# A third weight tile for the projections, loads one product further ahead, and two moved steps, in an encoder and decoder layer on one core

## The chip, the core and the metric

The kernel runs on 1 core of one Trainium2 chip. It is one program in which five engines work beside each other and wait for each other by semaphores: TensorE (PE, matrix products and transposes), VectorE (DVE), ScalarE (ACT), GpSimd (POOL) and SyncE (SP). SP only issues transfers: every transfer of this kernel is issued on SP, in the order in which the program writes them, and a transfer that waits for something holds back all those behind it. The metric is the device time of one execution in microseconds (us); of several runs the median is given. Everything is float32.

## The reference

The reference is one transformer layer pair with relative position biases, cut here to what is computed:

```python
x = src                                    # ctx_1024, (2, 77, 512)
n = ln(x, n1); x = x + mha(n, n, enc_in, enc_out, enc_bias)       # 16 heads of 32
x = x + relu(ln(x, n2) @ ff1.T + b1) @ ff2.T + b2                 # 512 -> 2048 -> 512
memory = x
y = tgt                                    # x, (2, 2048, 512)
n = ln(y, n1); y = y + mha(n, n, sa_in, sa_out, self_bias + causal)
y = y + mha(ln(y, n2), memory, ca_in, ca_out, cross_bias)
y = y + relu(ln(y, n3) @ ff1.T + b1) @ ff2.T + b2
```

The large part is the causal self-attention over 2048 tokens in two batches. The encoder works on 77 tokens only.

## The kernel before

**Two phases.** The decoder's 2 x 2048 tokens are cut into 8 blocks of 512 tokens (batch b, block m; x = 0 to 7 counts them through). The first phase does the self-attention of all blocks, and beside it the whole encoder, and the cross-attention of the very first block. The second phase does cross-attention and feed-forward of the eight blocks; it is a stream of products whose weights come through a ring of 16 tiles.

**Units and slots.** The first phase is cut into 128 units: a unit is 128 query rows of one group of four heads. A block has 16 units (4 groups by 4 row tiles); block x begins at unit 16x. For each unit, PE makes the scores in pieces of up to 512 keys (L374), DVE brings them from PSUM to SBUF, adds the bias to the last two tiles of keys and takes the maxima (L383, L390, L400), ACT takes the exponentials (L405), PE transposes them (L425), DVE and ACT copy the transposes out (L429, L431), and PE multiplies them with the values (L442). At the end of a unit the main loop calls `slot(n + 1)` (L1179), which runs the extra work hung on that slot, in this order: the entries of `light[n]`, then the jobs of `jobs[n]`, each with `load_next()` in front of it, then the entries of `late[n]`. So the program order of every engine, and of the transfers on SP, is written out by hand through the slot numbers.

**The products of the projections.** Queries, keys and values of a block are made by jobs: `q_job` and `k_job` (L216, L227) take a 512 x 128 piece of the weights; from the second block of a batch on, keys and values are made by seven products of 256 x 256 quarters instead of eight (`part_job`, L990; the table `PARTS` names for each product the weight's quarter, or a sum of quarters S1 to S4 kept in DRAM, and the tokens' quarter, or a sum T1 to T4). Below, k6 of block 6 is the sixth such product for the keys. The order of the products of a block x > 1 that starts at slot u is: q0 at u-5, k1 k6 at u-4, k7 k4 at u-3, k2 k5 at u-2, k3 v1 at u-1, v6 v7 at u, v4 v2 at u+1, then q1, v5 v3, q2 and q3 up to u+5. Block 1 has three in slot 17: v7, v4 and v2. Each of these products has a weight tile `wqk` of 128 x 512 f32 (256 KB), with two buffers in turn. The values of a batch's first block and the output projections use another, single weight tile of 1 MB (`wbig`) and count as jobs without a small tile.

**When a weight is loaded.** All jobs stand in one queue. In front of each job the loop `load_next` (L1127 to L1133) issues loads for the jobs that follow: up to job `ran + 2` (`ran` is the job about to run; a little further at the start), and no further than that two small tiles are in use from `ran` on. With two buffers, the load of a product is therefore written just ahead of the product before it, and has to wait until the product two before it has been read by PE.

**The encoder's steps.** `encoder()` (L489) yields 28 steps, one a slot. Step 15 centers the rows and adds the output bias row `row` on POOL (`add_row`, L632), and then loads the next row, `ca_bv`, into the same tile (`load_row`, L526), which waits for POOL to have read it. It is at the end of slot 16. Step 16, at the end of slot 17, turns the normed rows on PE (L554). The row `ca_bv` is read by step 27 (L748).

**The first cross block.** `first_cross()` (L858) spreads the first block's cross-attention over the slots 65 to 95. Its third layer norm writes each of four row tiles turned into one tile `slab` on ACT (L784, step 20 + 3t), and `store` (L920) sends the slab to `nT3_d` and the rows to `y1` in the same step, so in slots 85, 88, 91 and 94.

**A row tile.** `bv`, a tile of 2 KB per partition, holds the output bias of the cross-attention in the second phase (`early_loads`, L1217, slot 123; used through `norm_stages`, L776). Two `wqk` buffers serve as `o_sums` there, once the projections are done.

Of the kernel before, what the change touches and what calls it, by code (L numbers as in the profile page):

```python
# [17 lines left out]
P = 128  # L18
# [36 lines left out]
def tile_encoder_decoder(ctx: ExitStack, tc: tile.TileContext, ins, out):  # L55
# [103 lines left out]
    with (  # L159
# [12 lines left out]
        wbt = ac.tile([P, NC, D], F32, name="wbig")  # L172
        pts_all = ac.tile([P, 8, HC * P], F32, name="pts")
        oT_all = ac.tile([P, 6, TB * P], F32, name="oT")
        bv = ac.tile([P, D], F32, name="row_sa_bv")
        bo = ac.tile([P, D], F32, name="row_dec_sa_out_b")
        psum = ps.tile([P, 8, 512], F32, name="psum")
        count = {"bank": 0, "banks": 7, "pts": 0, "oT": 0, "mm": 0}
# [17 lines left out]
        wbig, xs, xr = {}, {}, {}  # L196

        def small_w(c0, name="dec_sa_in_wT"):
            w = sb.tile([P, NC, P], F32, name="wqk", tag="wqk", bufs=2)
            nc.sync.dma_start(w, wchunk(name, c0, P))  # L200
            return w

# [286 lines left out]
        def encoder():  # L489
# [218 lines left out]
            def stage():  # L708
                for b in range(B):
                    keep[b] = center(b)  # L710
                add_row()
                load_row("ca_bv")

            yield stage
            yield lambda: [turned(b, keep.pop(b), "n2") for b in range(B)]

            def first(i):
                project(ws["1", i], relu, i * NC)
# [139 lines left out]
        def first_cross():  # L858


            plan = {}

            def at(slot, f):
                plan.setdefault(slot, []).append(f)

            o = 2 * HC * MB
            ys = [pp[:, o + t * D : o + (t + 1) * D] for t in range(TB)]
            qT = pp[:, o + 2048 : o + 4096].rearrange("p (g n) -> p g n", n=MB)
            prs = [pp[:, o + 4096 + i * H * S : o + 4096 + (i + 1) * H * S] for i in range(2)]
            o += 4096 + 2 * H * S  # L870
            kTc = pp[:, o : o + NC * S].rearrange("p (c k) -> p c k", k=S)
            vc = pp[:S, o + NC * S : o + NC * S + D]
            slab = pp[:, o + NC * S + D : o + NC * S + 2 * D].rearrange("p (c n) -> p c n", n=P)
            assert o + NC * S + 2 * D <= 12288
            nT = pp[:, HC * MB : 2 * HC * MB].rearrange("p (c n) -> p c n", n=MB)
            wq, wo = vv[:, 8:12, :], vv[:, 12:16, :]
            rows = {"dec_ca_out_b": kT[:, 0, 3 * MB :], "dec_ff2_b": kT[:, 3, 3 * MB :]}
            oT, xn = kT[:, 1, 3 * MB :], kT[:, 2, 3 * MB :]

            def pts(g):  # L880
                return kT[:S, g, 2 * MB : 3 * MB]

            def loads():
                for t in range(TB):
                    nc.sync.dma_start(ys[t], y1[0][0][:, t, :])
                for n, row in rows.items():
                    i = _ROWS.index(n)
                    nc.sync.dma_start(row, ins["rows"][i : i + 1, :].to_broadcast([P, D]))
                nc.sync.dma_start(wq, wchunk("dec_ca_in_wT", 0))
                nc.sync.dma_start(kTc, ckT_d[:, :, :S])  # L890
                nc.sync.dma_start(vc, cv_d[:, 0, :])

            def more_loads():
                for i in range(2):
                    bias_tile(prs[i].rearrange("p (h k) -> p h k", k=S), 2, P, S, 255 - P * i)
                nc.sync.dma_start(wo, wchunk("dec_ca_out_wT", 0))

            at(0, loads)
            at(5, more_loads)
            for t in range(TB):  # L900
                y = lambda t=t: ys[t]
                fs = norm_stages(
                    y, "n2", rows["dec_ca_out_b"], lambda: xn, lambda t=t: nT[:, :, ts(t, P)]
                )
                for k, f in zip((0, 1, 2, 1), fs):
                    at(1 + t + k, f)
            for g in range(NC):
                at(7 + g, lambda g=g: q_group(g, wq[:, :, ts(g, P)], nT, qT[:, g, :]))
            for t in range(TB):
                y = lambda t=t: ys[t]  # L910
                fs = attend_stages(
                    lambda g, t=t: qT[:, g, ts(t, P)], kTc, vc, y, t < 2, prs[t % 2], pts, lambda: oT, wo
                )[:7]
                for k, f in zip((0, 1, 2, 2, 4, 5, 6), fs):
                    at(11 + 3 * t + k, f)
                fs = norm_stages(y, "n3", rows["dec_ff2_b"], lambda: xn, lambda: slab)
                for k, f in zip((0, 1, 2, 1), fs):
                    at(18 + 3 * t + k, f)

                def store(t=t):  # L920
                    nc.sync.dma_start(nT3_d[:, :, ts(t, P)], slab)
                    nc.sync.dma_start(y1[0][0][:, t, :], ys[t])

                at(20 + 3 * t, store)
            return plan


# [62 lines left out]
        def part_job(kind, b, m, i):  # L990
            name, by = PARTS[i]

            def load():
                w = sb.tile([P, NC, P], F32, name="wqk", tag="wqk", bufs=2).rearrange("p c o -> p (c o)")
                w = w.rearrange("p (c o) -> p c o", c=2)
                if name[0] == "S":
                    src = sa_d[kind][int(name[1]) - 1].rearrange("p (c o) -> p c o", c=2)
                else:
                    src = quarter("dec_sa_in_wT", int(name[1]) - 1, int(name[0]) - 1, sa_from[kind])
                nc.sync.dma_start(w, src)  # L1000
                return w

            def place(to):
                r, c = int(to[0]) - 1, int(to[1]) - 1
                if kind == "k":
                    return kT[:, 2 * r : 2 * r + 2, m * MB + c * TOK : m * MB + (c + 1) * TOK]
                return vv[:, m * TB + 2 * c : m * TB + 2 * c + 2, ts(r, TOK)]

            def run(w):
                n, mm = of_nT(b, m, by), bank()  # L1010
                left, right = (w, n) if kind == "k" else (n, w)
                for f in range(2):
                    for c in range(2):
                        nc.tensor.matmul(
                            mm[:, ts(f, TOK)], left[:, c, ts(f, P)], right[:, c, :], start=c == 0, stop=c == 1,
                        )
                got = mm.rearrange("p (f n) -> p f n", f=2)
                d = {to: place(to) for to in ("11", "12", "21", "22")}
                if i == 1 and kind == "k":
                    for f in range(2):  # L1020
                        nc.scalar.activation(
                            d["11"][:, f, :], got[:, f, :], AF.Identity, bias=vec("dec_sa_in_b", NC + f)
                        )
                elif i == 1:
                    nc.scalar.copy(d["11"], got)
                elif i == 6:
                    ve.tensor_tensor(d["12"], got, d["11"], ALU.add)
                elif i == 7 and kind == "k":
                    for f in range(2):
                        ve.scalar_tensor_tensor(  # L1030
                            d["22"][:, f, :], got[:, f, :], kstep[:, f : f + 1], d["12"][:, f, :], ALU.add, ALU.add
                        )
                elif i == 7:
                    ve.tensor_tensor(d["22"], got, d["12"], ALU.add)
                elif i == 4:
                    ve.tensor_tensor(d["21"], got, d["22"], ALU.add)
                else:
                    for to in ADDS[i]:
                        ve.tensor_tensor(d[to], got, d[to], ALU.add)

            return load, run, True
# [84 lines left out]

        def load_next():  # L1127

            while len(loaded) < min(len(queue), ran[0] + (5 if ran[0] < 4 else 3)):
                ahead = [queue[i][2] for i in range(ran[0], len(loaded) + 1)]  # L1130
                if sum(ahead) > 2:
                    break
                loaded.append(queue[len(loaded)][0]())  # L1133

# [81 lines left out]

        def early_loads():  # L1217
            nc.sync.dma_start(nTt, nT3_d)
            row_into(bv, "dec_ca_out_b")
            for o in range(2):  # L1220
                o_sums.append(sb.tile([P, NC, P], F32, name="wqk", tag="wqk", bufs=2).rearrange("p c o -> p (c o)"))

        def last_loads():
            t = sb.tile([P, MB], F32, name="q", tag="q", bufs=3)
# [10 lines left out]
                t = sb.tile([P, HC, 2 * P], F32, name="bias", tag="bias", bufs=2)  # L1235
                qT.append(t.rearrange("p (g a) k -> p g (a k)", g=2))

        xt_ring = []
        light[len(units) - 5].append(early_loads)
        light[len(units) - 1].append(last_loads)  # L1240

# [333 lines left out]
        def cross(x):  # L1575
# [8 lines left out]

            for t in range(TB):
                fs = norm_stages(
                    lambda t=t: y_of(x, t), "n2", bv, place("xt"), lambda t=t: nT2[:, :, ts(t, P)]
                )
                for k, f in zip((0, 2, 4, 11), fs):
                    plan[t + k].append(f)  # L1590
# [225 lines left out]
```

## Time and profile before

Three runs took 2823.34, 2816.31 and 2821.03 us, the median is 2821.03 us. The profiled execution took 2821.11 us; its span, from the first to the last instruction of the program, is 2819.2 us. So some 1.9 us lie around the span.

| engine | busy, us | share of the span |
|---|---|---|
| PE | 2771.8 | 98% |
| DVE | 1886.7 | 67% |
| ACT | 1440.2 | 51% |
| POOL | 915.1 | 32% |

The mean granted clock of TensorE is 0.992 of full speed, and the transfers move 129 GB/s over the span. A line such as `PE L1014 MATMUL psum<-xr,wqk 128*128 128x256 f32 x8 [1.74 <-DMA wqk<-in_dec_sa_in_wT_dram]` in the list by time reads: eight matmuls of line 1014 write PSUM from the tiles xr and wqk, and PE stood idle for 1.74 us before them, until the transfer into wqk had landed. In front of it stand the start and the length in us. In the list of waits a row names who waited, for whom, how long in all, how often, and the longest. SPq is SP's queue of transfers. PEclk is the granted clock.

### The profile page before, as it was taken

To read this page: it belongs to the slowest core of one execution; us is meant where nothing else is said; L and a number is where in the kernel's file an instruction comes from. 1 tells how busy PE (TensorE), PEld (TensorE's weight loads), DVE (VectorE), ACT (ScalarE), POOL (GpSimd) and SP (SyncE) were. 2 spreads that over 40 slices of the span, in tenths; PEclk is the share of its full clock that TensorE was granted. 3 is DMA by queue.
4 is the path that set the end of the run, shared out by engine and by line. 5 is a ranking of instruction groups with operands and counts; after the bars stand their busy time and mean duration, and the time that the engine had idled before them with its cause. 6 is when DMAs were issued, how large, how long until landed. Compare 5 with 4: busy or idle time off the path is not lost. (4 is left out here: it accounts for less than half of the span.)

```text
span 2819.2 us, 66842 instructions
## 1 busy us (share of the span) xinstructions
PE 2771.8 (98%) x26294; PEld 2146.2 (76%) x26294; DVE 1886.7 (67%) x5412; ACT 1440.2 (51%) x2761; POOL 915.1 (32%) x777
## 2 busy tenths in 40 slices
PE   9899999999999999999999999999999999999998
PEld 5567776677667566666677667898989898989898
DVE  4666588778886578678778886464646555564645
ACT  3534456656666556646665666425353434444431
POOL 1501124500100312211400001274746474747456
PEclk9999999999999999999999999999999999999999
DMA  7423345410111621232311013474748574746475
GB/s 218 138 67 124 97 128 158 144 58 24 43 39 56 164 76 50 80 106 83 114 49 34 28 47 126 150 246 142 248 139 252 157 236 157 228 158 224 146 227 181
DMA packets 282251, 362.45 MB, mean 129 GB/s; under 512 B 39072, under 2 KB 156624, under 8 KB 281810
## 3 DMA queue, kind: packets, MB, share of 16 engines
q1 hardware_dynamic: 281938, 358.18, 40.9%
q8 instruction: 208, 3.41, 0.5%
q14 instruction: 105, 0.86, 0.1%
HBM read 314.49 MB, written 43.59 MB: 127 GB/s over the span
## 5 line engine op out<-in xcount | busy, mean ns | idle before, releaser
L405 ACT ACTIVATE pp<-pp,nm 128x128 f32<-128x128 f32 (+15 forms) x512 | 612.0, 1202 | 132.9 <-DVE nm L400 132.4
L383 DVE TENSOR_SCALAR_CACHE_REDUCE pp<-psum 128x512 f32<-128x512 f32 (+3 forms) x1024 | 558.9, 590 | 57.9 <-PE psum L374 56.3
L431 ACT COPY pts<-psum 128x512 f32<-128x512 f32 (+3 forms) x592 | 301.4, 576 | 522.5 <-PE psum L425 399.1
L425 PEld LDWEIGHTS psum<-ident,pp 128*128 128x128 f32 x4352 | 478.2, 142 | 110.9 <-DVE pp L383 53.7
L425 PE MATMUL psum<-ident,pp 128*128 128x128 f32 x4352 | 540.2, 279 | 9.4 <-ACT pp L405 3.3
L429 DVE COPY pts<-psum 128x512 f32<-128x512 f32 (+2 forms) x544 | 330.1, 659 | 74.6 <-PE psum L425 74.2
L374 PE MATMUL psum<-kT,q 32*128 32x512 f32 (+3 forms) x2560 | 365.5, 578 | 4.9 <-DVE pp L383 2.9
L442 PEld LDWEIGHTS psum<-pts,vv 128*32 128x32 f32 x8704 | 225.6, 110 | 127.4 <-issue 116.7
L1518 PE MATMUL psum<-pp 128*128 128x128 f32 x2560 | 304.5, 276 | 1.9 <-POOL pp L932 1.6
L1518 PEld LDWEIGHTS psum<-pp 128*128 128x128 f32 x2560 | 296.3, 192 | 8.6 <-issue 2.8
L442 PE MATMUL psum<-pts,vv 128*32 128x128 f32 x8704 | 279.6, 275 | 2.4 <-DVE pts L429 1.7
L932 POOL TENSOR_TENSOR pp<-pp 128x512 f32<-128x512 f32 x159 | 212.6, 1354 | 129.3 <-DMA pp<-in_dec_ff_wT_dram 70.3
L1489 PE MATMUL psum<-vv,pp 128*128 128x256 f32 x1024 | 236.2, 381 | 0.0
L374 PEld LDWEIGHTS psum<-kT,q 32*128 32x128 f32 x2560 | 127.7, 184 | 125.7 <-issue 80.3
L1489 PEld LDWEIGHTS psum<-vv,pp 128*128 128x128 f32 x1024 | 190.3, 190 | 25.8 <-issue 0.5
L390 DVE CUSTOM_DVE_ANT_0 pp<-psum,bias 128x256 f32<-128x256 f32 (+1 forms) x512 | 196.1, 411 | 15.6 <-PE psum L374 15.5
L1502 DVE TENSOR_TENSOR kT<-kT,psum 128x512 f32<-128x512 f32 x96 | 65.8, 686 | 191.1 <-PE psum L1489 190.9
L1489 PE MATMUL psum<-nT,pp 128*128 128x256 f32 x768 | 174.1, 380 | 0.0
L1505 ACT ACTIVATE kT<-kT,vecs 128x256 f32<-128x256 f32 x192 | 87.0, 501 | 156.7 <-DVE kT L1502 156.1
L470 POOL TENSOR_TENSOR oT<-rirows,oT 128x512 f32<-128x512 f32 x30 | 38.3, 1275 | 387.7 <-DMA rirows<-rec 239.3
L1489 PEld LDWEIGHTS psum<-nT,pp 128*128 128x128 f32 x768 | 144.2, 190 | 20.3 <-issue 1.6
L1526 ACT COPY oT<-psum 128x128 f32<-128x128 f32 x56 | 15.0, 267 | 239.0 <-PE psum L1518 239.0
(242 smaller groups left out, 3915.8 us busy)
## 6 DMA issues: line engine op xcount, KB each, us to landing
pp<-w_d SPq DMA_DIRECT2D x520, 256.0 KB
pp<-in_dec_ff_wT_dram SPq DMA_DIRECT2D x112, 256.0 KB
wqk<-in_dec_sa_in_wT_dram SPq DMA_DIRECT2D x76, 256.0 KB
bias<-tzg SPq DMA_DIRECT2D x128, 128.0 KB
pp<-wo_d SPq DMA_DIRECT2D x56, 256.0 KB
vv<-in_enc_ff_wT_dram SPq DMA_DIRECT2D x8, 1024.0 KB
xr<-in_x_dram SPq DMA_DIRECT2D x32, 256.0 KB
vv<-y SPq DMA_DIRECT2D x32, 256.0 KB
```

The lines of the kernel that those rows point to most:

```text
L374: nc.tensor.matmul(banks[r][:, : kn * P], q[rows4(r), ts(t, P)], kT[rows4(r), g, k0 * P : (k0 + kn) * P], start=True, stop=True,)
L383: nc.vector.tensor_scalar(p[:, k0 * P : (k0 + far) * P], s[:, : far * P], 1.0, None, ALU.mult, ALU.max, accum_out=st["mx"][:, r, c : c + 1],)
L390: nc.vector.tensor_tensor_reduce(p[:, (i + 1) * P - w : (i + 1) * P], s[:, far * P : kn * P], biases[b, m, g][:, r, 2 * P - w :], 1.0, LOW ...
L405: nc.scalar.activation(p, p, AF.Exp, bias=nm, accum_out=to)
L425: nc.tensor.transpose(pt[:, ts(x, P)], state[n]["p"][r][:, ts(k, P)], ident)
L429: nc.vector.tensor_copy(pts[:, : len(load), :], pt[:, :w])
L431: nc.scalar.copy(pts[:, : len(load), :], pt[:, :w])
L442: nc.tensor.matmul(ot[rows4(r), t, :], vv[:, k, ts(g * HC + r, HD)], got.pop((n, k, r)), start=(k == 0), stop=(k == i),)
L932: engine.tensor_tensor(out, a, b, ALU.subtract)
L1489: nc.tensor.matmul(mm[:, ts(f, TOK)], a[:, c, ts(f, P)], b[:, c, :], start=fresh and f == 0 and c == 0, stop=c == 1, skip_group_check=True,)
L1505: nc.scalar.activation(dst[:, e, :], src[:, e, :], AF.Relu, bias=vec("dec_ff1_b", f + e))
L1518: nc.tensor.matmul(psum[:, bank_i, ts(col, P)], lhs[:, c, :], w[:, c, :], start=fresh and k in (0, 3) and c == 0, stop=c == 3, skip_group_ ...
```

## The change

- The tile `wqk` gets a third buffer, everywhere it is taken. The room comes from the tile `bv`, which goes: its row is now loaded, at the same place, into a `wqk` buffer (`row_ca`).
- `load_next` looks one job further (`ran + 3`) and lets three small tiles be in use.
- The load of the row `ca_bv` moves from the encoder's step 15 to the end of its step 16, so from the end of slot 16 to the end of slot 17.
- The first cross block's stores move one slot later: 86, 89, 92 and 95.

```diff
-        bv = ac.tile([P, D], F32, name="row_sa_bv")
...
         def small_w(c0, name="dec_sa_in_wT"):
-            w = sb.tile([P, NC, P], F32, name="wqk", tag="wqk", bufs=2)
+            w = sb.tile([P, NC, P], F32, name="wqk", tag="wqk", bufs=3)
...
                 add_row()
+
+            yield stage
+
+            def stage():
+                for b in range(B):
+                    turned(b, keep.pop(b), "n2")
                 load_row("ca_bv")
 
             yield stage
-            yield lambda: [turned(b, keep.pop(b), "n2") for b in range(B)]
...
-                at(20 + 3 * t, store)
+                at(21 + 3 * t, store)
...
             def load():
-                w = sb.tile([P, NC, P], F32, name="wqk", tag="wqk", bufs=2).rearrange("p c o -> p (c o)")
+                w = sb.tile([P, NC, P], F32, name="wqk", tag="wqk", bufs=3).rearrange("p c o -> p (c o)")
...
-            while len(loaded) < min(len(queue), ran[0] + (5 if ran[0] < 4 else 3)):
+            while len(loaded) < min(len(queue), ran[0] + (5 if ran[0] < 4 else 4)):
                 ahead = [queue[i][2] for i in range(ran[0], len(loaded) + 1)]
-                if sum(ahead) > 2:
+                if sum(ahead) > 3:
                     break
...
         def early_loads():
             nc.sync.dma_start(nTt, nT3_d)
-            row_into(bv, "dec_ca_out_b")
+            row_ca.append(sb.tile([P, NC, P], F32, name="wqk", tag="wqk", bufs=3).rearrange("p c o -> p (c o)"))
+            row_into(row_ca[0], "dec_ca_out_b")
             for o in range(2):
-                o_sums.append(sb.tile([P, NC, P], F32, name="wqk", tag="wqk", bufs=2).rearrange("p c o -> p (c o)"))
+                o_sums.append(sb.tile([P, NC, P], F32, name="wqk", tag="wqk", bufs=3).rearrange("p c o -> p (c o)"))
...
-                    lambda t=t: y_of(x, t), "n2", bv, place("xt"), lambda t=t: nT2[:, :, ts(t, P)]
+                    lambda t=t: y_of(x, t), "n2", row_ca[0], place("xt"), lambda t=t: nT2[:, :, ts(t, P)]
```

More of the change, by code (lines that the diff above doesn't have):

```diff
@@ L1236, in late_loads @@
                 qT.append(t.rearrange("p (g a) k -> p g (a k)", g=2))
-        xt_ring = []
+        xt_ring, row_ca = [], []
         light[len(units) - 5].append(early_loads)
```

## The prediction

> **What bounds the kernel now.** I read the page first, then the list of waits of PE, then the list by time around each long wait, on PE and on SP.
>
> ```profile
> span 2819.2 us, 66842 instructions
> ## 1 busy us (share of the span) xinstructions
> PE 2771.8 (98%) x26294; PEld 2146.2 (76%) x26294; DVE 1886.7 (67%) x5412; ACT 1440.2 (51%) x2761; POOL 915.1 (32%) x777
> ```
>
> PE has work in 98% of the span, so it stands idle for 2819.2 - 2771.8 = 47.4 us. Only what is in those 47.4 us, or makes PE's own work slow, can be won by moving loads. PE's list of waits names who ends the idle time:
>
> ```profile
> PE psum L1014 <- DMA wqk<-in_dec_sa_in_wT_dram: 8.1, 4, 5.0
> PE psum L1014 <- DMA wqk<-sa_k: 7.5, 2, 6.2
> PE psum L425 <- ACT pp L405: 3.3, 4, 1.2
> ...
> PE psum L425 <- ACT nT L311: 2.2, 2, 1.4
> ...
> PE psum L216 <- DMA wqk<-in_dec_sa_in_wT_dram: 1.6, 1, 1.6
> ```
>
> Seven waits for a weight tile `wqk` make 8.1 + 7.5 + 1.6 = 17.2 us, by far the largest cause; the next one, the exponentials, has 3.3 us in four pieces. PE's list by time shows where the seven stand:
>
> ```profile
> 93.08 3.67 PE L216 MATMUL psum<-nT,wqk 128*128 128x512 f32 x8 [1.64 <-DMA wqk<-in_dec_sa_in_wT_dram]
> ...
> 136.73 1.97 PE L1014 MATMUL psum<-xr,wqk 128*128 128x256 f32 x8 [1.34 <-DMA wqk<-sa_k]
> ...
> 181.15 3.75 PE L1014 MATMUL psum<-wqk,xr 128*128 128x256 f32 x8 [4.99 <-DMA wqk<-in_dec_sa_in_wT_dram]
> 184.69 2.06 PE L1014 MATMUL psum<-wqk,nT 128*128 128x256 f32 x8
> ...
> 353.76 1.89 PE L1014 MATMUL psum<-xr,wqk 128*128 128x256 f32 x8
> 357.39 1.97 PE L1014 MATMUL psum<-xr,wqk 128*128 128x256 f32 x8 [1.74 <-DMA wqk<-in_dec_sa_in_wT_dram]
> 359.28 1.14 PE L374 MATMUL psum<-kT,q 32*128 32x512 f32 x8
> ...
> 1015.45 1.97 PE L1014 MATMUL psum<-xr,wqk 128*128 128x256 f32 x8 [1.11 <-DMA wqk<-in_dec_sa_in_wT_dram]
> ...
> 1197.27 1.97 PE L1014 MATMUL psum<-xr,wqk 128*128 128x256 f32 x8 [0.29 <-DMA wqk<-in_dec_sa_in_wT_dram]
> ...
> 1213.72 3.75 PE L1014 MATMUL psum<-xt,wqk 128*128 128x256 f32 x8 [6.20 <-DMA wqk<-sa_k]
> 1217.40 2.03 PE L374 MATMUL psum<-kT,q 32*128 32x512 f32 x8
> ```
>
> Two stand out, 4.99 us at 181 (block 1's v4, slot 17) and 6.20 us at 1213 (block 6's k5, slot 94). The eight matmuls behind them take 3.75 us, where the same eight take 1.89 us at 353.76. The granted clock in those stretches tells why; the third row is the product behind the 1.74 us wait (columns: stretch, length, busy time of PE, PEld, DVE, ACT, POOL with counts, PEclk, share and GB/s of the transfers):
>
> ```profile
> 178.19:185.02 6.83, 3.87 (x9) 3.19 (x10) 0.08 (x1) 0.04 (x1) 0.00 (x0) 0.50 0.36 111
> 1212.43:1219.26 6.83, 5.54 (x16) 3.04 (x16) 1.29 (x2) 0.00 (x0) 0.00 (x0) 0.50 0.26 83
> 357.39:359.28 1.89, 1.89 (x8) 1.40 (x8) 0.00 (x0) 0.21 (x2) 0.00 (x0) 1.00 0.64 214
> ```
>
> In both long waits the clock fell to 0.50 and stayed there for 6.83 us; behind the short one it is 1.00. In both long stretches DVE, ACT and POOL had hardly any work (0.08 and 1.29 us of DVE), so nothing else was being caught up: the whole kernel stood.
>
> **Where the change meets this: the third tile.** From the code: with two buffers the load of product j is written ahead of product j-1 and waits for j-2 to be read. With three, and one job further ahead, it is written ahead of j-2 and waits for j-3. In both versions that is the product just in front of the place where the load is written. So SP stands at the same places for the same products, and what is queued behind those waits waits no longer than now; but each tile is asked for a whole product, mostly a whole slot, earlier. By this rule k5 of block 6 is written in slot 93 (behind k7) instead of slot 94, and v4 of block 1 in slot 16 instead of slot 17.
>
> SP's list by time shows what that is worth:
>
> ```profile
> 166.24 0.32 SPq L1000 DMA_DIRECT2D wqk<-sa_v  x1
> 172.78 0.32 SPq L526 DMA_DIRECT2D pp<-in_rows_dram  x1
> 173.15 2.67 SPq L463 DMA_DIRECT2D rec<-rt  x4
> 175.86 1.87 SPq L342 DMA_DIRECT2D bias<-tzg  x4
> 177.83 0.91 SPq L1000 DMA_DIRECT2D wqk<-in_dec_sa_in_wT_dram  x2
> ...
> 1208.95 0.58 SPq L921 DMA_DIRECT2D nT_d<-pp  x1
> 1209.63 0.56 SPq L922 DMA_DIRECT2D y<-pp  x1
> 1210.28 1.00 SPq L1000 DMA_DIRECT2D wqk<-sa_k  x2
> ```
>
> At 181, v4's load leaves at 177.83, behind the row load `ca_bv` that left at 172.78 and the eight transfers of slot 17. After the change it stands where v7's load stands now, 166.24, some 10 us before PE could use it (v7 ends about 181.15 - 4.99 = 176.16). At 1213, k5's load leaves at 1210.28, behind the store that SP had to wait for. A load takes about 1213.72 - 1210.28 = 3.4 us from there to PE; written in slot 93, behind the load of 1197.27's product, it leaves some 8 us before PE wants it at 1213.72 - 6.20 = 1207.52.
>
> **Where it meets this: the two moved steps.** SP's own waits name both:
>
> ```profile
> SPq L921 <- ACT pp L784: 28.4, 4, 9.6
> ...
> SPq L526 <- POOL pp L632: 6.1, 1, 6.1
> ```
>
> The row load waits 6.1 us for POOL's addition. One step later it is written behind `rec` (4 transfers), `bias` (4) and the weight loads of slot 17, all of which it held back; POOL is done by 172.78, before SP gets there, so the new place waits for nothing. Its only reader comes in slot 28, eleven slots later. Neither moved step issues anything on POOL; the steps' PE and DVE work stays where it is. The four pairs of stores wait 28.4 us for ACT's slab, 9.6 us of it at 1208.95. One slot later each is written behind two weight loads and the slot's small transfers, and the slab is written by then; the slab's next writer is now two slots off instead of three (slots 93 and 94 stand 16.4 us apart above, at 1197.27 and 1213.72), against 3.4 us for such a 256 KB transfer. I cost the store's delay at nothing, because nothing reads `y1` and `nT3_d` before slot 123. Without that cover, one late slab would cost ACT at most one such transfer, 3.4 us.
>
> **What it adds.** The number of loads is the same; the row of `bv` only goes elsewhere, into a `wqk` tile whose last product ran at least six slots before. At the start, the load of the second q-product moves from 17.62 to ahead of the first bias tile:
>
> ```profile
> 11.89 1.92 SPq L342 DMA_DIRECT2D bias<-tzg  x4
> ...
> 17.62 0.39 SPq L200 DMA_DIRECT2D wqk<-in_dec_sa_in_wT_dram  x1
> ...
> 25.11 0.28 DVE L390 CUSTOM_DVE_ANT_0 pp<-psum,bias 128x128 f32<-128x128 f32 x1
> ```
>
> It puts 0.39 us of issue and one transfer, at most 3.4 us, ahead of a bias tile that is used 25.11 - 13.81 = 11.3 us later. Cost 0; if that cover were gone, up to 3.8 us, once.
>
> **The sum.** Wait at 1213: 6.20, and the slow clock behind it (3.75 - 1.89) + (2.03 - 1.14) = 2.75, together 8.95 us. Wait at 181: 4.99 + (3.75 - 1.89) + (2.06 - 1.89) = 7.02 us. The shorter waits of the seven-product scheme: 1.34 + 1.74 + 1.11 + 0.29 = 4.48 us (bounds 0 and 4.48, if exponentials or a drain would be late next; I take all, since in the long ones the other engines had nothing left to catch up with). The wait at 93: bounds 0 and 1.64 us. Soon behind it PE waits for the token norm (ACT nT L311, 2.2 us in the list of waits), whose chain of loads and statistics does not come earlier; I take 0. Sum 8.95 + 7.02 + 4.48 = 20.45 us. The profiled execution took 2821.11 us, 0.08 us from the median of the runs, so the sum holds for both: 2821.11 - 20.45 = 2800.7 us.
>
> What is late next: exponentials.
>
> ```profile
> 1209.83 1.04 ACT L405 ACTIVATE pp<-pp,nm 128x896 f32<-128x896 f32 x1
> ```
>
> That is the last of its unit at 1213; it ends at 1210.87. With k5 at 1207.52, PE would come to the transposes that read it after k5 (1.89), scores (1.14), values and scores again, past 1212, so there is about a microsecond of room.
>
> [...] The trace shows clock 0.50 behind waits of 4.99 and 6.20 us and 1.00 behind one of 1.74 us. [...]
>
> **The rivals.**
>
> *The half clock elsewhere moves* (this is also the case that ends slower). Five more stretches show clock 0.50:
>
> ```profile
> 642.40:649.23 6.83, 6.83 (x28) 5.01 (x25) 5.26 (x19) 2.02 (x4) 0.00 (x0) 0.50 0.01 2
> ...
> 1492.32:1499.15 6.83, 6.83 (x27) 4.88 (x25) 5.27 (x17) 2.46 (x4) 0.00 (x0) 0.50 0.00 0
> sum 30.72, PE 29.83 PEld 24.57 DVE 18.60 ACT 15.35 POOL 10.26; mean PE 5.97 PEld 4.92 DVE 3.72 ACT 3.07 POOL 2.05
> ```
>
> They last 30.72 us together, in steps of 3.41 us (9 of them), with PE busy for 29.83 us of them but fed in small pieces; each step costs up to 1.7 us. The changed program runs up to 20 us earlier there, so steps may go or come. If all go, 15.4 us more are won: 2785.3 us. For no change, 20.45 / 1.7 = 12 new steps are needed; for slower by 0.3% (8.5 us), 17, so 2830 us. Against it: the two rows shown are alike and one batch apart (850 us), so the work, not chance, places them. [...]
>
> *Only the moved steps act.* If the third tile were of no use, because SP still got to each load no sooner, the moves alone would free the two long waits, 8.95 + 7.02 = 15.97 us: 2805.1 us. That the short waits come back as waits for ACT or DVE gives the same time.
>
> *The loads are hidden anyway, or the freed time is taken by the next wait.* Then it would end within 0.3% (8.5 us, about what a measurement of this kernel can tell from no change). Against it stand the idle DVE, ACT and POOL above. One of the two long waits would have to stay whole, and the short ones too: 2821.11 - 8.95 = 2812.2 us or more.
>
> **How the numbers follow.** The forecast, all but the wait at 93 gone, with three clock steps more or less (5.1 us): 2795 to 2806 us, chance 0.64. Most clock steps gone as well, 2785 to 2795 us: 0.10. The part that only the moves bring, or a little less, 2806 to 2812.5 us: 0.11. Within 0.3%: 0.09. Slower, by clock steps: 0.06. Faster is 0.64 + 0.10 + 0.11 = 0.85. The range 2788 to 2812 us leaves out the slower and the unchanged case and a part of the first one.
>
> **What would show it right or wrong.** Right: no wait of PE for `wqk` above 0.5 us; the stretches of half clock near 178 and 1212 gone; SP's wait L526 for POOL gone and L921's 28.4 us below 8; PE idle about 47.4 - 15.7 = 32 us; DVE's, ACT's and POOL's busy times unchanged. Wrong: a PE wait for exponentials (L405) or drains (L383) of several us where the long waits were; new stretches of clock 0.50; the first bias tile late near 25 us.

## The result and the profile after

Five runs of the changed kernel took 2793.78 to 2797.37 us, the median is 2794.67 us; five of the kernel before beside them have a median of 2822.97 us (2816.31 to 2825.05). The ratio is 0.9906, with a 95% interval of 0.9892 to 0.9921: about 0.9% faster, inside the range and 6.0 us below the forecast of 2800.7 us. The profiled execution took 2795.96 us, its span is 2794.2 us, 25.0 us shorter than the span before.

The page's first part, of the changed kernel (its lines are numbered a little higher: L1018 is L1014 before, L925 is L921, L310 is L311):

```profile
span 2794.2 us, 66837 instructions
## 1 busy us (share of the span) xinstructions
PE 2762.3 (99%) x26294; PEld 2141.1 (77%) x26294; DVE 1885.7 (67%) x5412; ACT 1439.3 (52%) x2761; POOL 915.1 (33%) x777
```

PE's idle time fell from 47.4 to 2794.2 - 2762.3 = 31.9 us, and its busy time by 2771.8 - 2762.3 = 9.5 us, although it does the same 26294 matmuls. DVE, ACT and POOL worked as long as before. PE's list of waits, from its top:

```profile
PE psum L424 <- ACT pp L404: 3.3, 4, 1.2
PE psum L373 <- ACT nT L310: 2.7, 2, 2.1
PE psum L373 <- DVE pp L382: 2.5, 5, 1.0
PE psum L424 <- ACT nT L310: 2.3, 2, 1.4
PE psum L424 <- ACT pts L430: 2.0, 2, 1.5
```

No weight tile stands in it any more; before, three rows of it made 17.2 us. PE's list by time at the two places where the long waits were:

```profile
172.14 3.62 PE L1018 MATMUL psum<-wqk,xr 128*128 128x256 f32 x16
175.59 1.89 PE L1018 MATMUL psum<-wqk,nT 128*128 128x256 f32 x8
...
1191.86 1.89 PE L1018 MATMUL psum<-nT,wqk 128*128 128x256 f32 x8
1193.59 1.89 PE L1018 MATMUL psum<-xt,wqk 128*128 128x256 f32 x8
1195.41 1.14 PE L373 MATMUL psum<-kT,q 32*128 32x512 f32 x8
```

v7 and v4 run as one row of sixteen matmuls, v2 follows at once; k2, k5 and the scores too, all at full speed (1.89 and 1.14 us, where the products took 3.75 and the scores 2.03). SP's list by time shows the loads at the first of the two places:

```profile
164.87 0.38 SPq L1004 DMA_DIRECT2D wqk<-in_dec_sa_in_wT_dram  x1
165.35 2.68 SPq L462 DMA_DIRECT2D rec<-rt  x4
168.07 1.88 SPq L341 DMA_DIRECT2D bias<-tzg  x4
170.05 0.40 SPq L1004 DMA_DIRECT2D wqk<-in_dec_sa_in_wT_dram  x1
174.06 0.39 SPq L199 DMA_DIRECT2D wqk<-in_dec_sa_in_wT_dram  x1
175.79 0.34 SPq L1004 DMA_DIRECT2D wqk<-sa_v  x1
176.22 0.35 SPq L525 DMA_DIRECT2D pp<-in_rows_dram  x1
```

v4's load leaves at 164.87, not at 177.83 behind the row load, and v2's at 170.05; the row load goes out at 176.22 behind the weights. At the second place k5's load is the one from `sa_k` at 1183.77, 9.8 us before k5 starts at 1193.59, and the store comes two slots later:

```profile
1183.77 0.34 SPq L1004 DMA_DIRECT2D wqk<-sa_k  x1
...
1195.18 0.58 SPq L925 DMA_DIRECT2D nT_d<-pp  x1
```

**Where the time came from.** The matmuls are the same 26294 in the same order in both traces. So for each of them the start before minus the start after is the lead that the changed kernel has there, and every place where the lead grows or shrinks can be read. In us, with the terms of the prediction and the traces of the experiments below, all against the trace of before:

| place (old time) | forecast | changed | again (e5) | tile only (e1) | moves only (e2) |
|---|---|---|---|---|---|
| wait at 93 | 0 | +1.80 | +1.80 | +1.80 | -1.38 |
| behind it, 93 to 125 | - | -1.38 | -0.77 | -1.90 | -1.25 |
| wait at 137 | 1.34 | +1.50 | +1.50 | +1.51 | -0.19 |
| wait at 181, with the slow clock | 7.02 | +7.14 | +7.14 | +2.48 | +5.71 |
| wait at 357 | 1.74 | +1.90 | +1.90 | +1.90 | +0.32 |
| wait at 1015 | 1.11 | +1.27 | +1.27 | +1.27 | -0.10 |
| wait at 1197 | 0.29 | +0.45 | +0.45 | +0.45 | +0.45 |
| wait at 1213, with the slow clock | 8.95 | +9.12 | +9.12 | +9.12 | +9.12 |
| all the rest | 0 | +3.21 | +2.08 | +4.64 | +0.91 |
| span | 20.45 | 25.01 | 24.49 | 21.27 | 13.59 |

The seven weight waits gave 23.18 us in both executions of the changed kernel. That they agree says that no such wait is left in either; their sizes all come from the one trace of before. "All the rest" of the first execution is the start (+1.0 us), four steps of half clock that came or went (+1.0 us together, with what PE got back behind them) and pieces of less than half a microsecond each (+1.2 us).

### The profile page after: what moved, and what is told of

The parts are those of the page before. It is cut to its first block, busy times and chain, and to the rows that moved or that the text cites. A ratio compares the mean times of both kernels' runs of the same rounds, so it can differ in the third digit from the quotient of the medians.

```text
span 2794.2 us, 66837 instructions
## 1 busy us (share of the span) xinstructions
PE 2762.3 (99%) x26294; PEld 2141.1 (77%) x26294; DVE 1885.7 (67%) x5412; ACT 1439.3 (52%) x2761; POOL 915.1 (33%) x777
## 3 DMA queue, kind: packets, MB, share of 16 engines
q8 instruction: 208, 3.41, 0.5%
```

## The experiments

The theory was that a product waited because its load stood late in SP's order, and that a long wait also halves PE's clock. Rivals were that only the moved steps act on the long waits, that the missing buffer and not the order made the loads late, and that the slow products have another cause than the wait.

**The third tile without the moves.** The changed kernel with both steps put back:

```diff
                 add_row()
+                load_row("ca_bv")
 
             yield stage
-
-            def stage():
-                for b in range(B):
-                    turned(b, keep.pop(b), "n2")
-                load_row("ca_bv")
-
-            yield stage
+            yield lambda: [turned(b, keep.pop(b), "n2") for b in range(B)]
...
-                at(21 + 3 * t, store)
+                at(20 + 3 * t, store)
```

> The third tile and the longer look-ahead, both moved steps undone. Order theory (a product waited because its load was written late on SP, behind something that SP had to wait for): k5 of block 6 is written one slot ahead of the store that held it back, so the 6.20 us wait and its slow clock are gone, and so are the short ones. In slot 17 the row load again stands ahead of v2's load, which leaves near 177.8 on the old time and lands near 181.2, wanted near 178: a wait of about 3 us is left. Span 2794.2 + 3 = 2797 us. Rival (only the moves act on the two long waits): both stay, span near 2819.2 - 4.5 = 2815 us, and only the short waits go.

Measured 2802.01 us, ratio 0.9933 (0.9918 to 0.9948), span 2797.9 us. PE's list by time, and the clock in the step that holds most of the wait and in the next one:

```profile
179.17 3.42 PE L1013 MATMUL psum<-wqk,nT 128*128 128x256 f32 x8 [2.96 <-DMA wqk<-in_dec_sa_in_wT_dram]
```

```profile
175.31:178.72 3.41, 0.90 (x5) 0.45 (x3) 0.69 (x1) 1.26 (x4) 0.00 (x0) 1.00 0.93 261
178.72:182.13 3.41, 2.96 (x7) 2.45 (x8) 0.00 (x0) 0.00 (x0) 0.00 (x0) 0.50 0.74 203
```

The wait at 1213 is gone as a whole without the store's move, and at 181 the one wait forecast is left: v2, 2.96 us. It also cost one step of half clock; 7.14 - 2.48 = 4.66 us is 2.96 + 1.70. So the rival falls, and the row load's move is worth 4.7 us at this place beside the third tile. The runs' ratios, 0.9933 here and 0.9906 for the changed kernel, lie some 7.6 us apart; they hold whatever else differed between the executions.

**The moves without the third tile.** The kernel before with the two moved steps only.

> Two tiles and the look-ahead of before, with both moved steps. Order theory: the two long waits and their slow clock go (about 8.95 + 7.02 us by the terms of the prediction), the short waits stay (4.48 us, and about 1 us at 93), and v2 in slot 17, whose load has to wait for v7 with two tiles, waits about 1.5 us. Span about 2819.2 - 16 + 1.5 = 2805 us, between 2800 and 2807. Rival (the moves do nothing without the third tile): 2815 us or more.

Measured 2807.16 us, ratio 0.9951 (0.9936 to 0.9966), span 2805.6 us. PE's list of waits:

```profile
PE psum L1019 <- DMA wqk<-in_dec_sa_in_wT_dram: 3.8, 3, 1.4
PE psum L216 <- DMA wqk<-in_dec_sa_in_wT_dram: 3.5, 2, 3.0
```

The two long waits are gone (5.71 and 9.12 us in the table), the short ones stay, but for the one of 0.29 us at 1197. The one at 93 was longer than before, 3.02 us. The moves can't have done that: both steps come in slot 16 or later, so up to 93 this is the kernel before. So are the two filled kernels below, and there the same wait is 2.47 and 1.63 us. It differs between executions of the same program, and the 1.80 us that the table gives for it are as uncertain.

So the wait at 1213 needed two things, a load written behind the store and a store that stood there, and taking away either is enough: 9.12 us each way. At 181 the moves alone give 5.71 of 7.14 us, the tile alone 2.48, and only both the whole. The forecast's rival "only the moved steps act" gets its size, too: 2807.16 us, where 2805.1 us had been worked out for it.

**The buffer without the order.** Three buffers, but the look-ahead and the steps of before. The edit of the look-ahead, against the changed kernel:

```diff
-            while len(loaded) < min(len(queue), ran[0] + (5 if ran[0] < 4 else 4)):
+            while len(loaded) < min(len(queue), ran[0] + (5 if ran[0] < 4 else 3)):
...
-                if sum(ahead) > 3:
+                if sum(ahead) > 2:
```

> A third buffer alone: the look-ahead and the two moved steps are those of before, so every load is written where it was, but waits for a product one further back. Order theory: the place on SP is what makes a load late, so nearly all of the seven waits stay, and the span is 2816 to 2819 us. Rival (the missing buffer made the loads late): the short waits go and the long ones shrink, span below 2812 us.

Measured 2817.68 us, ratio 0.9995 (0.9985 to 1.0005), span 2815.5 us. PE's list of waits:

```profile
PE psum L1013 <- DMA wqk<-sa_k: 6.8, 1, 6.8
PE psum L1013 <- DMA wqk<-in_dec_sa_in_wT_dram: 6.4, 2, 4.8
```

A third buffer alone changes no time that can be measured. The long waits and the one at 357 stay, for their loads are written behind something that SP waits for. Three short ones went, at 137, 1015 and 1197 (1.51, 1.28 and 0.45 us by the lead), which I had not expected: there the load did wait for its buffer. At 93 a wait of 1.77 us is left; this profile puts it down to DVE. So the order holds the large part, and the buffer a part of the short waits.

**The waits filled with idle work.** The kernel before, with transposes of the identity into the next PSUM bank in front of the two products that wait longest; no load moves:

```diff
+        fill = {23: 28, 123: 38}
+
...
                 load_next()
+                if ran[0] in fill:
+                    warm(fill[ran[0]])
                 run(loaded[ran[0]])
```

> The kernel before, with idle transposes of the identity put in front of the two products that wait longest: 28 in slot 17 (about 3.8 us of 4.99) and 38 in slot 94 (about 5.2 us of 6.20). No load moves. Clock theory: PE's standing still halves the clock, and that costs (1.86 + 0.17) + (1.86 + 0.89) = 4.8 us beside the waits; with work in the wait the clock stays, the two stretches of 0.50 near 178 and 1212 vanish, and the span is 2819.2 - 4.8 = 2814.4 us though both products start when they did. Rival (the products behind the waits are slow for another reason, the clock only goes with it): no gain, span 2819 us or a little more.

Measured 2819.4 us, ratio 0.9992 (0.9982 to 1.0002), span 2814.5 us; in time that is no difference. The trace tells more: v4 ran in 1.97 us (full clock) behind a wait left of 1.68 us, but at the other place the 38 transposes took only 4.31 us, a wait of 2.20 us was left, and one step of half clock came all the same. So it was run again with more of them (40 and 54):

> As the filled kernel, with 40 and 54 idle transposes instead of 28 and 38, so that hardly any of the two long waits is left empty. In the first filling the product behind the 4.99 us wait ran at full clock, while behind the other a wait of 2.20 us was left and one step of half clock came. Clock theory: with 54 the second product runs at full clock too, in 1.9 us instead of 2.71, and the scores behind it in 1.14 instead of 2.04; both stretches of half clock are gone. Rival: the second stays slow. In time it is worth at most 4.8 us against the kernel before, near what five rounds can tell.

Measured 2816.7 us, ratio 0.9984 (0.9976 to 0.9993), span 2811.4 us. PE's list by time, and the two stretches' clock:

```profile
174.81 4.53 PE L1147 MATMUL psum<-ident 128*128 128x128 f32 x40
181.02 1.97 PE L1014 MATMUL psum<-wqk,xr 128*128 128x256 f32 x8 [1.68 <-DMA wqk<-in_dec_sa_in_wT_dram]
182.82 1.89 PE L1014 MATMUL psum<-wqk,nT 128*128 128x256 f32 x8
...
1203.20 6.06 PE L1147 MATMUL psum<-ident 128*128 128x128 f32 x54
1210.39 1.96 PE L1014 MATMUL psum<-xt,wqk 128*128 128x256 f32 x8 [1.12 <-DMA wqk<-sa_k]
1212.28 1.14 PE L374 MATMUL psum<-kT,q 32*128 32x512 f32 x8
```

```profile
178.19:185.02 6.83, 5.15 (x35) 4.48 (x33) 0.69 (x1) 0.00 (x0) 0.00 (x0) 1.00 0.32 101
1208.00:1215.00 7.00, 5.88 (x80) 4.22 (x82) 2.54 (x7) 0.00 (x0) 0.00 (x0) 1.00 0.40 114
```

Both products still start when their loads land, and now run in 1.97 and 1.96 us instead of 3.75, the scores in 1.14 instead of 2.03. With work in the wait the clock stayed at 1.00 in both stretches, so that PE's standing still cost the slow clock at these two places is shown. Matmul by matmul the two places gained 1.91 and 2.68 us behind the waits, 4.6 us of the 4.78 (2.03 + 2.75 us, the slow products of the two places before). The medians differ by 2821.79 - 2816.7 = 5.1 us (by the interval, 2 to 7 us). That this comes out so near is partly luck: the two loads landed 1.0 and 0.8 us later in this trace, and steps of half clock elsewhere, near 482 and 1333, went as well.

**The changed kernel again, and without the store's move.** Side by side on one chip; the second only puts `at(20 + 3 * t, store)` back.

> The changed kernel once more, unaltered, on the chip of the three runs beside it. Expected near 2795 us and 25 to 28 us under the kernel before. Its trace tells which of the gains of the first trace come back: those by the weight waits (near 93, 136, 181, 357, 1015, 1197 and 1213 on the old time) should agree within 0.3 us; the steps of half clock near 163, 250, 482 and 1333 may fall otherwise if the clock's window alone places them.

> The changed kernel with only the first cross block's stores put back to their old slot. Order theory: with the third tile nothing that PE waits for is written behind the store, so the store's move is worth nothing beside it: same time as the changed kernel within 2 us, and no wait for a weight tile. Rival (the store's move is what freed the 6.20 us wait): about 9 us slower than the changed kernel.

Measured 2794.24 us (0.9906, 0.9892 to 0.9921) and 2792.80 us (0.9903, 0.9889 to 0.9916). The seven weight waits gave the same 23.18 us in both traces. The store's move is worth nothing beside the third tile; the version without it has the lowest median of all, but 1.4 us can't be told from nothing here. The half clock, whose window is the step of 3.41 us that the traces show, fell otherwise: in the second execution of the changed kernel the step near 163 came again, the one near 259 did not, and the one near 482, gone in the first, was there.

**The next wait.** The longest wait left is for ACT's copies in the second block's token norm. Half of them on DVE:

```diff
-                if c or not apart:
+                if (c % 2 if (b, m) == (0, 1) else c or not apart):
```

> The changed kernel, with half of the copies out of PSUM in the second block's token norm (two of four for each row tile) done on DVE instead of ACT. After the weight waits these copies are what PE waits for longest near 109 to 118 us (5.0 us in four waits), ahead of a stretch of half clock. If ACT's queue is the cause, about 3 us of the waits go, and perhaps the stretch of half clock: 2789 to 2792 us. Rival (the order of the slots is the cause, the wait then stands on DVE): no gain.

Measured 2795.09 us, ratio 0.9908 (0.9894 to 0.9921): no gain. Its list of waits shows 2.3 + 2.0 us for ACT's copies still:

```profile
PE psum L373 <- ACT nT L310: 2.3, 2, 1.5
PE psum L424 <- DVE mx L389: 2.1, 3, 1.5
PE psum L424 <- ACT nT L310: 2.0, 2, 1.3
```

The 2.1 us for DVE are no effect of the edit: the second trace of the changed kernel has the same row. The two waits that the changed kernel's trace has as 1.41 and 0.84 us, near 110, are 1.30 and 0.74 us here. In both traces the copies start behind the exponentials in ACT's order, at 107.84, so halving their number hardly moved when PE could go on.

## Why the prediction was right

**The bound** was read rightly: what went is PE's idle time at the weight tiles and the slow clock behind it, and no other engine took it over, but for a piece at 93 (below).

**The order on SP.** "Each tile is asked for a whole product, mostly a whole slot, earlier" holds: v4's load left at 164.87, near the 166.24 forecast, and k5's in slot 93, a slot before the store's old place. That the places where SP stands stay the same fits: PE waits for no transfer any more, and the first bias tile was in time.

**The two long waits.** 8.95 and 7.02 us were forecast, 9.12 and 7.14 us came. The slow clock behind them, 2.75 + 2.03 = 4.78 us of it, was right in cause and nearly in size: filling the waits brought it back without moving a load.

**The short waits.** 4.48 us were taken, 5.12 us came (1.50 + 1.90 + 1.27 + 0.45), 0.16 us more at each. That is how a wait is counted: from the end that the profile gives the product before it. Without a wait the next product begins 0.16 us ahead of that end (k2 above: 1191.86 + 1.89 = 1193.75, and k5 begins at 1193.59).

**The wait at 93** was mis-sized. "I take 0" was the step: 1.80 us went, and PE gave back 1.38 and 0.77 us of it in the two executions. The reason held, that the token norm's chain does not come earlier, but not the place. PE's two longest waits for the norm's copies (ACT nT L311 before) stayed at 1.41 and 0.84 us. What grew is DVE's wait for the norm's row, 2.1 us in the first execution instead of 0.7, and behind it PE's next wait at the transposes, here before and after:

```profile
DVE bnst L283 <- DMA xr<-in_x_dram: 0.7, 1, 0.7
99.60 0.30 PE L425 MATMUL psum<-ident,pp 128*128 128x128 f32 x1 [0.71 <-DVE mx L390]
...
DVE bnst L282 <- DMA xr<-in_x_dram: 2.1, 1, 2.1
98.06 0.30 PE L424 MATMUL psum<-ident,pp 128*128 128x128 f32 x1 [1.45 <-ACT pts L430]
```

The second execution has the same 1.45 us there, put down to DVE. That DVE's wait causes PE's is read from the order of these rows; no run tried it.

**The half clock elsewhere.** The sum of these stretches fell only from 30.72 to 27.31 us, one step:

```profile
159.74:163.15 3.41, 3.41 (x17) 3.35 (x16) 2.79 (x15) 1.55 (x3) 0.00 (x0) 0.50 0.02 5
...
sum 27.31, PE 25.92 PEld 20.42 DVE 18.45 ACT 9.33 POOL 6.92; mean PE 5.18 PEld 4.08 DVE 3.69 ACT 1.87 POOL 1.38
```

Steps near 482 and 1333 went (+1.45 and +1.67 us), new ones came near 163 and 259 (-1.67 and -1.56 us, of which 0.75 and 0.40 us came back right behind them). So the price, up to 1.7 us a step (half of 3.41 us), holds, and the rival moved the span by about 1 us in this execution. But the argument against it, that the work and not chance places them, held only for some: the stretch near 642 came in all ten traces of this study, the one near 482 in one of the two executions of the changed kernel. So the 25.0 us of the traces are the 20.45 us of the sum, 2.73 us more at the seven waits (23.18 - 20.45), 1.38 us given back, and 3.21 us of all the rest. The rest was no part of the forecast: that it comes out at a few us of gain is luck. The medians of the runs lie 28.3 us apart, and the interval of their ratio, 22 to 30 us, holds the 25.0.

**The moved steps.** The row load: right, its wait for POOL is gone and it freed v2. The store: its cost of nothing was right (the kernel without its move took 2792.80 us), but "below 8" for its wait was wrong, as was the claim that the slab is written by then:

```profile
SPq L925 <- ACT pp L788: 14.4, 3, 9.2
```

The 9.2 us are the third store's, and they are 9.2 us in the trace of before and with the moves only, too. There, nothing stands on SP between the old place and the new one: in all three traces the issue just ahead of this store is the same `y<-xr` (L255 in the changed kernel, L256 in the others). So "behind two weight loads and the slot's small transfers" was wrong for this store. The fourth, the one ahead of k5 before, fell from 9.6 to 1.0 us. No wait of PE for a weight follows any of them.

## What to carry to other kernels

When PE waits for a load, look first at what stands ahead of the load in its queue: a buffer alone changed nothing that could be measured (0.9995), the same buffer with the loads written one product earlier gave 0.9933. A wait of PE can cost more than its length (here 4.99 us cost 7.14, and behind one of 1.77 us, in the trace with the buffer alone, the clock was 0.50), so price it with the slow products behind it. Compare traces matmul by matmul: the terms of one pair of traces then come out to 0.1 us, where the runs' times spread over several us; but a wait's size in a single trace is one execution's. Where a wait needs two things at once, undo each alone before either is called the cause.

## What the runs showed of the hardware

In these traces the clock was halved behind waits shorter than one of its steps. In the ten traces the granted clock changes only at the borders of steps of 3.41 us, on one grid through a whole trace. Behind a wait of 2.96 us (tile only) it fell to 0.50, and so it did behind one of 1.77 us (buffer only), while behind one of 3.02 us with the moves only it stayed at 1.00:

```profile
91.75 5.37 PE L215 MATMUL psum<-nT,wqk 128*128 128x512 f32 x8 [1.77 <-DVE bnmv L283]
```

```profile
93.97 3.24 PE L216 MATMUL psum<-nT,wqk 128*128 128x512 f32 x7 [3.02 <-DMA wqk<-in_dec_sa_in_wT_dram]
```

The traces tell the three apart. Cut along each trace's own grid, the first is the two rows shown with the tile-only kernel; the other two are (buffer only, then moves only):

```profile
88.75:92.17 3.42, 1.65 (x11) 1.12 (x10) 2.62 (x14) 2.67 (x10) 3.31 (x4) 1.00 0.96 295
92.17:95.58 3.41, 3.41 (x5) 1.33 (x4) 1.29 (x4) 0.06 (x1) 3.41 (x3) 0.50 0.13 33
...
89.12:92.53 3.41, 1.75 (x15) 1.27 (x12) 1.92 (x10) 2.53 (x9) 3.30 (x3) 1.00 0.83 265
92.53:95.95 3.42, 1.98 (x5) 1.05 (x6) 2.60 (x7) 0.28 (x2) 3.42 (x3) 1.00 0.44 143
95.95:99.36 3.41, 3.41 (x45) 1.65 (x45) 1.68 (x2) 1.23 (x1) 2.82 (x3) 1.00 0.03 5
```

The wait of 2.96 us left PE idle for 3.41 - 0.90 = 2.51 us of one step, the one of 1.77 us lies whole in one step, and the one of 3.02 us is spread over two, 1.66 and 1.44 us. It is the idle time within one step that sorts these cases, not the wait's length. In all ten traces the clock fell to 0.50 behind each of the sixteen full-clock steps with 1.77 us of idle time or more; three of these are in the trace of before, with 1.83, 2.04 and 3.41 us from 109.92, 174.78 and 1209.02 on. Of the 26 with 1.3 to 1.71 us it fell behind six, all near 107 to 116 us, at the second block's token norm; in the changed kernel it is the step from 111.95 on, with 1.33 us. The wait of 1.74 us at 357 in the kernel before left 1.71 us in its step and the clock behind it stayed at 1.00. Idle time does not sort all of them: the stretch near 642 follows a step with 0.2 to 0.33 us of it (0.33 us in the trace of before). This is read from the traces; no run set out to try it.
